# A graph convolution and attention kernel: attention moved from behind the second pass into it

## The chip, the cores and the metric

The kernel runs on one core of one Trainium2 chip. The metric is device time in microseconds (us). TensorE (PE) multiplies matrices, with its weight loads (PEld) shown apart; VectorE (DVE) and ScalarE (ACT) work on elements; GpSimd (POOL) issues the indirect transfers, that is gathers and scatters by a list of row numbers; SyncE (SP) and the queue of ACT issue the other transfers. Each engine works through its own list of instructions in order, and semaphores tie the lists together.

## The reference

N = 12500 nodes with D = 256 features, E = 200000 edges sorted by their destination. H = 4 heads of C = 64. Cut to what matters:

```
h = relu(layernorm(x))
h = h @ W_pre + b_pre                    # with a self loop added for each node:
h = relu(gcn(h, W1, b1)); h = relu(gcn(h, W2, b2))
x = x + h @ W_post + b_post
#   gcn(h): out[dst] += (h @ W)[src] * dinv[src] * dinv[dst];  + b
h = relu(layernorm(x)); xt = (h @ weight).reshape(N, 4, 64)
alpha_l = einsum('ehd,hd->eh', xt[src], attn_l)     # one score per edge and head
alpha_r = einsum('ehd,hd->eh', xt[dst], attn_r)
alpha = softmax(leaky_relu(alpha_l + alpha_r, 0.01), axis=1)      # over the 4 heads
tmp = einsum('nh,nhd->nd', alpha[:N], xt[dst[:N]])  # only the first N edges count
out = x + broadcast(tmp over the 4 heads)
```

So the attention needs, for each of the first 12500 edges, a score of its source, which can be any node, and the row of its destination. As the edges are sorted, the destinations of these edges are among the first nodes only (XW node tiles), while the sources spread over all 98.

## The kernel before

Edges are taken in tiles of 128 and chunks of J = 14 tiles: 112 chunks, 1563 tiles. Nodes are in NT = 98 tiles of 128.

A prologue normalises x, counts degrees, and writes the scaled rows to a table in DRAM. It also computes statistics of the rows of chunk 0 that were gathered raw from x (`raw_stats`, a bn_stats and a bn_aggr for each of 14 tiles).

Then `convolve` runs twice, once per graph convolution. For each edge tile POOL gathers the 128 source rows into a row buffer (L1397); for each chunk DVE makes a matrix of ones and zeros that marks the destinations (`fhot`, L1243); PE multiplies the two into the chunk's sum (`facc`, L1407). At the end of a chunk, `close` turns that sum and adds it to a moving buffer of node sums (L1288, L1208, L1305). A node tile whose sum is complete goes through `finish1` or `finish2`, whose steps are put off by a fixed number of edge tiles (the list at the end of `finish2`) and are carried out by `run(t)` after each tile. The order of every engine's list is thus written out by the loop over the tiles: what is emitted at tile t stands behind all that was emitted before.

In pass 1, chunks 0 to 3 were gathered raw in the prologue (RAW = 4; their statistics are taken one chunk ahead, at j = 9 of the chunk before), and chunks 4 to 27 are gathered as float32 rows of ftable. Meanwhile `split_rows` reads each node tile of that table back, splits it into three bf16 parts whose sum is the float32 value, and stores them (parts1). From chunk SINCE = 28 on, gathers take the parts and three bf16 matmuls do the work of a float32 one. Pass 2 takes parts for all chunks, from parts2, which `finish1` wrote. The row buffers of pass 2 are 4 of 9 tiles; those of the float32 part hold 14 tiles each. A gather into a row buffer waits until PE has multiplied what the buffer held before.

`finish2` ends with x after the two convolutions (fx, stored to kept_x by SP, L1563 and L1565), its normalised row, and the product with wg, which holds the attention weights (q, L1597): for node tiles under XW the whole row and its right score (table_r), for all the left scores, which ACT stores to table_l and table_e (r, L1605). table_e is table_l without the last three node tiles, so that the first chunk's gathers need not wait for them. During pass 2 `set_up` loads the sources and destinations that the attention starts with, and the rows of the first 14 tiles of the attention are multiplied out (`ends`, L1623).

The attention stands behind pass 2. It works on the 98 tiles of the first 12500 edges, in groups of G = 7. `ends_of` gets the destinations' rows by a product of a one-hot (`hot_t`, L1642) with rows that POOL gathered (`own_rows`, L1647): fends, L1741. `mix` has POOL gather the left scores of each tile's sources (fal, L1751), adds the scores that the three last node tiles lack in table_e (`missing`, L1722), takes the softmax (L1757 to L1767), weighs and sums the four heads on DVE (L1774 to L1781), adds the result to the kept x (fres, L1783) and stores it. The core of it:

```
for g in range(len(groups) + 2):
    if g < len(groups):
        keep(g)
        ends_of(g)
    if g >= 2:
        mix(g - 2)
```

Of the kernel before, what the change touches and what calls it, by code (L numbers as in the profile page):

```python
# [17 lines left out]
P = 128  # L18
# [395 lines left out]
def fast_path(  # L414
# [64 lines left out]
    assert AC * J == NT and AC * CE <= E and XW < NT  # L479
    table_r = dram.tile([XW * P, DR], F32, name="table_r")  # L480
    table_l = dram.tile([NT * P, H], F32, name="table_l")

    LW = 3
    table_e = dram.tile([NT * P, H], F32, name="table_e")
# [18 lines left out]
    base_b = const.tile([P, NCH], F32, name="base_b")  # L503
    row_i = const.tile([P, AC], I32, name="row_i")
# [88 lines left out]
    with tc.tile_pool(name="fprep", bufs=1) as prep:  # L593
# [233 lines left out]
        with tc.tile_pool(name="fpsum", bufs=2, space=PSUM) as psum, \  # L827
# [208 lines left out]
            raw_stats(0)  # L1036
            due.append((len(blocks), late))
            while n_stats < NG or due:
                if to_scale and to_scale[0] + 1 < n_stats:
                    scale(False)  # L1040
                one_more()
                fetch(2)
                if due:
                    norms(due.pop(0)[1])
# [10 lines left out]
            wide = prep.tile([NCH, P], F32, name="wide")  # L1055
            nc.vector.tensor_copy(wide, base.to_broadcast([NCH, P]))
# [7 lines left out]
            nc.tensor.matmul(fk[:, 2, :NCH], wide, ident[:NCH, :NCH], start=True, stop=True)  # L1064
# [7 lines left out]
            for f in after:  # L1072
                f()
            after = [raw_block(ends, m, psum.tile([P, 4 * P], F32, name="ft"), j0)
                     for j0 in (8, 12)]
            nc.vector.tensor_copy(base_b, fk[:, 2, :NCH])
            nc.vector.tensor_scalar(row_i, base_b[:, :AC], lane, float(XW * P - 1), op0=ALU.add,
                                    op1=ALU.min)
# [16 lines left out]
    def check_chunks(work, psum):  # L1095
# [20 lines left out]
        kept = work.tile([1, 1], F32, name="n_kept", bufs=1)  # L1116
        nc.vector.tensor_reduce(kept, pt[:1, 2, :NCH], AX.X, ALU.add)
        nc.vector.tensor_add(kept, kept, counted)
        nc.vector.tensor_scalar(bad_row, kept, -1.0, float(NCH + 1), op0=ALU.mult, op1=ALU.add)
# [12 lines left out]
    def load_late(pool):  # L1132

        nc.scalar.dma_start(roots, root_t)
        for t, w in ((wb, w2), (wo, w_post), (wg[:, :, :D], w_gat)):
            nc.scalar.dma_start(t, w.rearrange("(k p) n -> p k n", p=P))
        nc.scalar.dma_start(b2c, b2.rearrange("(k p) -> p k", p=P))
# [8 lines left out]
    def late_weights(pool, attn):  # L1146

        for i, ar in enumerate(attn):
            for k in range(KC):
                prod = pool.tile([P, H, C], F32, name="fprod", bufs=1)  # L1150
                nc.vector.tensor_mul(prod.rearrange("p h c -> p (h c)"), wg[:, k, :D], ar)
                nc.vector.tensor_reduce(wg[:, k, D + i * H:D + (i + 1) * H], prod, AX.X,
                                        ALU.add)

    def convolve(ep, table, stride, width, ahead, with_sum, psum, prepare, finish, parts, since,
                 lacking=False, raw=(), rows_p=None, behind=None):
# [35 lines left out]

        def new_buf():
# [24 lines left out]
        for n0 in range(0, BW, P):  # L1218
            v, n = {}, min(P, BW - n0)
            new_turned(v)  # L1220
            turn_sums(load_rows(n0, n), 0, v)
            nc.vector.tensor_copy(state["buf"][0][:, :, n0:n0 + n], v["pt"][:, :KC, :n])
            if with_sum:
                nc.vector.tensor_copy(state["buf"][1][:, n0:n0 + n], v["ps"][:, 0, :n])
# [6 lines left out]
        ready(0)  # L1231


        const_p = psum.tile([P, P if with_sum else P + D], F32, name="iota_p", bufs=1)
        iota_p = const_p[:, :P]
        nc.vector.tensor_copy(iota_p, iota_w)
        if not with_sum:
            state["bias"] = const_p[:, P:]
            nc.vector.tensor_copy(state["bias"], bob)

# [21 lines left out]
        def new_rows_of():  # L1262
            if with_sum:
                return new_got()
            return rows_p.tile([P, ONE, 3 * stride], BF16, name="fgot", bufs=ahead)

        def late_sums():
# [3 lines left out]
            froms = new_rows_of().rearrange("p j d -> p (j d)")[:, :J * D]  # L1271
            froms = froms.rearrange("p (j d) -> p j d", d=D)
            assert stride == TW * P and D == TW * P
            for i in range(TW):
                one_hots(froms[:, :, i * P:(i + 1) * P], from_0[:, i, :])
            px = psum.tile([P, KC, P], F32, name="fpt", bufs=1)
# [86 lines left out]
        def raw_ahead(c, j):  # L1363
# [4 lines left out]
            elif j in (3, 5, 7, 9):  # L1368
                raw_block(raw_lohi[c], raw_m[c], fpt(), 2 * (j - 3))()
                if j == 9:  # L1370
                    raw_stats(c)
# [5 lines left out]
        for t, (c, j) in enumerate(tiles):  # L1377
# [4 lines left out]
            if many == 1:  # L1382
                if j == 0:
                    gots = (raw + [spare])[c] if raw and c <= len(raw) else new_rows_of()
                got = gots[:, j, :]
            else:
                i = (t - since * J) % ONE
                if i == 0:
                    gots = new_rows_of()
                    if since:  # L1390
                        gots = gots.rearrange("p j d -> p (j d)").bitcast(BF16)
                        gots = gots[:, :ONE * 3 * stride].rearrange("p (j d) -> p j d", j=ONE)
                got = gots[:, i, :]
# [16 lines left out]
            if some and j == nj[c] - 1:  # L1410
                for i in range(TW):
                    nc.tensor.matmul(acc, late[0][:, i, :], late[1][i], start=False,
                                     stop=(i == TW - 1))
            if j == nj[c] - 1:
# [3 lines left out]
            if behind:  # L1418
                behind(t)
            run(t)  # L1420
        run()
# [51 lines left out]
    def split_rows(pool, psum):  # L1473
        rows = {}

        def load(w):
            rows[w] = pool.tile([P, D1], F32, name="frow", bufs=4)
            nc.sync.dma_start(rows[w], table1[w * P:(w + 1) * P, :])

        def step(t):  # L1480
# [3 lines left out]
            if k < NT:  # L1484
                load(k)
            if k >= 2:
                p = psum.tile([P, 4, P], F32, name="fpt", bufs=1)
# [354 lines left out]
```

## Time and profile before

| | us |
|---|---|
| three runs | 4912.08, 4915.13, 4934.78 (median 4915.13) |
| the profiled execution | 4877.83 |
| its span | 4875.9 |
| PE, PEld busy | 2648.6, 1780.7 |
| DVE, ACT busy | 1387.0, 614.7 |
| POOL busy | 3109.7 |
| granted TensorE clock, mean | 0.682 |

The span can be read in stages by the gather line. The first gather of pass 1 starts at 135.3 us, the first with parts at 674.9, the first of pass 2 at 2378.6, the last one at 4625.6. The attention's own gathers start at 4670.1. In the table of busy time by stretch each row gives a stretch, its length, and for every engine its busy time and number of instructions. In a row of the gather line stand the number of instructions, the least, median and largest duration in ns, and the first and last start in us. "issue" as a releaser is time in which the engine waited for nothing that the profile shows; "remote" is a releaser that it can't name. Below 0.5% of the time, two measurements can't be told apart.

### The profile page before, as it was taken

The numbers are of one execution on the slowest core, as the hardware profiler recorded it, in microseconds if no ns is written. First come the engines' busy times: TensorE is split into PE (matmuls) and PEld (weight loads), VectorE is DVE, ScalarE is ACT, GpSimd is POOL, SyncE is SP. The second block draws the span as 40 slices with busy tenths as digits, with TensorE's granted clock in tenths as the row PEclk, the third lists the DMA queues.
The fourth block names the chain that finished last, engine by engine and source line by source line (L and its number), as shares of the span: only waits on it lengthen the run. The fifth ranks groups of instructions, "written<-read, shape, count | busy, mean of one in ns | idle before, by whom it ended". The sixth has DMA issues, their size and how long they took to land. (4 is left out here: it accounts for less than half of the span.)

```text
span 4875.9 us, 38956 instructions
## 1 busy us (share of the span) xinstructions
PE 2648.6 (54%) x13306; PEld 1780.7 (37%) x13306; DVE 1387.0 (28%) x3009; ACT 614.7 (13%) x1625; POOL 3109.7 (64%) x3299
## 2 busy tenths in 40 slices
PE   5756555555555555555545555545455555545553
PEld 4534433233233333333333334333333343434341
DVE  7445532112122222222222222222222222212236
ACT  5212210000000000000001100010111101101011
POOL 7566646666666666666566666666666666666643
PEclk7766666666666666666666667666676766767766
DMA  8566655555555555555556666565566666656635
GB/s 269 147 178 184 191 157 154 159 158 161 163 156 161 158 162 157 160 157 163 147 157 177 162 159 155 158 161 151 154 159 160 157 156 156 163 153 158 159 110 155
DMA packets 413533, 787.28 MB, mean 161 GB/s; under 512 B 101005, under 2 KB 267172, under 8 KB 413324
## 3 DMA queue, kind: packets, MB, share of 16 engines
q0 software_dynamic: 197264, 594.53, 46.8%
q1 hardware_dynamic: 170214, 173.89, 11.4%
q10 hardware_dynamic: 45846, 16.27, 1.3%
q8 instruction: 107, 1.75, 0.2%
q14 instruction: 102, 0.84, 0.1%
HBM read 692.31 MB, written 92.05 MB: 161 GB/s over the span
## 5 line engine op out<-in xcount | busy, mean ns | idle before, releaser
L1397 POOL DMA_INDIRECT fgot<-parts,fsrc_t x2720 | 2580.2, 949 | 1372.9 <-issue 783.2
L1407 PE MATMUL facc<-fgot,fhot 128*128 128x256 bf16 (+2 forms) x8986 | 1743.4, 335 | 1152.0 <-issue 1105.8
L1407 PEld LDWEIGHTS <-fhot 128*128 128x128 bf16 x8202 | 902.3, 113 | 1593.5 <-issue 1399.0
L1243 DVE TENSOR_TENSOR fhot<-iota_p,to_t 128x1792 bf16<-128x1792 f32 (+1 forms) x224 | 449.2, 2005 | 8.0 <-remote 8.0
L1397 POOL DMA_INDIRECT fgot<-ftable,fsrc_t x336 | 318.8, 949 | 184.0 <-issue 104.2
L1468 DVE TENSOR_TENSOR fpo<-fpo,fparts 128x256 f32<-128x256 f32 x97 | 41.8, 431 | 922.8 <-ACT fo L1454 704.4
L1549 DVE SCALAR_TENSOR_TENSOR fy<-rb,fb2c,fpz 128x128 f32<-128x128 f32 x194 | 58.7, 344 | 850.4 <-remote 677.6
L1305 DVE TENSOR_TENSOR buf<-buf,fturn 128x256 f32 x224 | 94.4, 421 | 699.1 <-remote 510.0
L1558 PE MATMUL fpo<-fwo,fz 128*128 128x256 f32 x388 | 149.2, 523 | 200.1 <-ACT fz L1552 126.8
L1288 ACT ACTIVATE fsums<-facc 128x257 f32<-128x257 f32 (+1 forms) x224 | 85.2, 380 | 1326.9 <-remote 1122.2
L1563 DVE SCALAR_TENSOR_TENSOR fx<-fpo,fdinv,fxb 128x256 f32<-128x256 f32 x97 | 46.9, 483 | 643.4 <-remote 366.9
L1407 PEld LDWEIGHTS facc<-fgot,fhot 128*128 128x128 f32 x784 | 179.4, 237 | 131.2 <-issue 98.1
L1445 PE MATMUL fpo<-wf,buf 128*128 128x256 f32 x388 | 149.2, 496 | 125.5 <-issue 82.3
L1542 PE MATMUL fpz<-buf,fwb 128*128 128x128 f32 x776 | 137.4, 327 | 117.6 <-issue 99.5
L1558 PEld LDWEIGHTS fpo<-fwo,fz 128*128 128x128 f32 x388 | 91.3, 261 | 233.1 <-ACT fz L1552 142.6
L1208 PE MATMUL fturn<-fident,fsums 128*128 128x128 f32 x448 | 118.4, 348 | 100.2 <-issue 52.4
L1542 PEld LDWEIGHTS fpz<-buf,fwb 128*128 128x128 f32 x776 | 121.7, 236 | 127.4 <-issue 104.4
L1208 PE MATMUL fturn<-fident,self 128*128 128x128 f32 x396 | 106.6, 352 | 82.5 <-issue 46.7
L1445 PEld LDWEIGHTS fpo<-wf,buf 128*128 128x128 f32 x388 | 87.9, 248 | 161.5 <-issue 99.1
L1597 PE MATMUL fpx<-fwg,ht 128*128 128x4 f32 (+1 forms) x388 | 69.2, 286 | 129.9 <-ACT ht L1588 99.0
L1751 POOL DMA_INDIRECT fal<-table_l,fsrc_t x84 | 80.5, 958 | 69.3 <-DVE fs L1758 44.6
L1208 PEld LDWEIGHTS fturn<-fident,fsums 128*128 128x128 f32 x448 | 70.7, 177 | 144.8 <-issue 75.4
(284 smaller groups left out, 2272.8 us busy)
## 6 DMA issues: line engine op xcount, KB each, us to landing
fgot<-parts,fsrc_t POOLq DMA_INDIRECT x2720
parts<-frow_p SPq DMA_DIRECT2D x98, 195.0 KB
parts<-fparts SPq DMA_DIRECT2D x98, 192.0 KB
frow<-ftable SPq DMA_DIRECT2D x98, 130.0 KB
self<-ftable SPq DMA_DIRECT2D x99, 128.0 KB
self<-ftable SPq DMA_DIRECT2D x97, 130.0 KB
ftable<-fo ACTq DMA_DIRECT2D x98, 128.0 KB
kept_x<-fx SPq DMA_DIRECT2D x98, 128.0 KB
```

Of the source, the lines that this page charges most:

```text
L1208: nc.tensor.transpose(v["pt"][:, i * KC + k, :], rows[:, k * P:(k + 1) * P], ident)
L1243: nc.vector.tensor_tensor(h, iota_p[:, None, :].to_broadcast([P, n, P]), to[:, :, None].to_broadcast([P, n, P]), ALU.is_equal)
L1288: nc.scalar.activation(sb, acc, AF.Copy)
L1305: nc.vector.tensor_add(b, b, v["pt"][:, :KC, :])
L1397: nc.gpsimd.indirect_dma_start(out=got, out_offset=None, in_=rows_of[:(NT - TW) * P, :] if some else rows_of[:], in_offset=bass.IndirectOf ...
L1407: nc.tensor.matmul(acc, hots[c][:, j, :], got[:, i * stride:i * stride + width], start=(j == 0 and i == 0), stop=(j == nj[c] - 1 and i == ...
L1445: nc.tensor.matmul(po, buf[:, k, :P], wf[:, k, :], start=(k == 0), stop=False)
L1542: nc.tensor.matmul(pz[:, m, :], wb[:, k, m * P:(m + 1) * P], buf[:, k, :P], start=(k == 0), stop=(k == KC - 1))
L1549: nc.vector.scalar_tensor_tensor(y[:, m, :], v["root"], b2c[:, m:m + 1], v["pz"][:, m, :], op0=ALU.mult, op1=ALU.add)
L1558: nc.tensor.matmul(po, v["z"][:, m, :], wo[:, m, :], start=(m == 0), stop=(m == KC - 1))
L1597: nc.tensor.matmul(px, v["ht"][:, k, :], wg[:, k, d0:], start=(k == 0), stop=(k == KC - 1))
L1751: nc.gpsimd.indirect_dma_start(out=al[:, i, :], out_offset=None, in_=(table_l if c else table_e)[:], in_offset=bass.IndirectOffsetOnAxis(a ...
```

## The change

1. Prologue. The statistics of raw chunk 1 are taken in the prologue's last loop instead of in chunk 0 of pass 1. Two small results that only the old attention used (base_b, row_i) go. In pass 1 the first rows are loaded before chunk 0 as before, but turned and added (`begin_sums`, `ready(0)`) after its 14th tile.
2. Pass 1. `split_rows` has two row buffers instead of four and issues a tile's load after the store of the tile two before. When the split is done, `list_late` makes, out of the first N edges, a packed list of the late ones: those whose source is in node tile 84 or later (LATE), in up to 16 lists of 128. It writes to DRAM the sources modulo 128 (lo_rows), the destinations less each tile's first (rel_rows), the lists and the start rows. Its 62 parts stand two tiles apart.
3. Pass 2. The row buffers are 3 of 14 tiles. The tables table_l and table_e and their stores go: the left scores stay in SBUF (l_all). `attend` gives a list of items; `feed(t)` starts an item when the node tiles that it needs are finished and the item before has had its space of edge tiles, and puts its parts at tiles t, t + 1 and so on. The items: a load of the destination rows of each of the 98 tiles (`ends_of_tile`, a register read on SP and a transfer of 128 x 260 B); alpha_r by a one-hot of the destinations (14 items); one-hots and destination rows of the late lists, written to DRAM (4 and 16 items); alpha_l in five stages over the source tiles 0 to 18, 18 to 36, 36 to 54, 54 to 72 and 72 to 84, each of 14 items (a broadcast load of 229 KB, a one-hot of 128 x 896 on DVE, 21 bf16 matmuls with the scores as three parts, a mask, a product and a reduction on DVE). The first four stages' items stand four tiles apart. The items of the last stage go on to the end (`group`, ten tiles apart): softmax, shares as three bf16 parts, spread by matmuls with `pick`, weighed one-hots, 7 float32 matmuls that mix, the sum with kept x, and the store.
4. Behind pass 2 only the late edges remain. Their one-hots (1 MB) and rows (2 MB) are loaded into freed row buffers, POOL gathers their 16 x 128 rows of kept x, 16 matmuls give the left scores of the last 14 node tiles, then mask, softmax and mix, and POOL scatters the 16 lists of finished rows over those in the output.

The diff, cut to its core:

```diff
-                    raw_stats(c)                      # pass 1, j == 9
+                    if c > 1:
+                        raw_stats(c)
+                if known < 2:                         # prologue's last loop
+                    raw_stats(known)
+                    known += 1
...
+            if with_sum and t == J - 1:
+                begin_sums()
+                ready(0)
...
+        def feed(t):
+            if behind and t >= free_at[0] and behind[0][0]():
+                _, space, parts = behind.pop(0)
+                for i, part in enumerate(parts):
+                    if part:
+                        at(t + i, lambda _, part=part: part())
+                free_at[0] = t + space
...
-            return rows_p.tile([P, ONE, 3 * stride], BF16, name="fgot", bufs=ahead)   # ahead 4
+            return rows_p.tile([P, J, 3 * stride], BF16, name="fgot", bufs=ahead)     # ahead 3
...
-            rows[w] = pool.tile([P, D1], F32, name="frow", bufs=4)
+            t = pool.tile([P, G * P], BF16, name="list_h", bufs=2)
+            rows[w] = t.bitcast(F32)[:, :D1]
...
-            nc.scalar.dma_start(table_l[w * P:(w + 1) * P, :], xa[:, DR:])
-            if w < NT - LW:
-                nc.scalar.dma_start(table_e[w * P:(w + 1) * P, :], xa[:, DR:])
+            nc.scalar.activation(l_all[:, w, :], v["px"][:, DR - d0:], AF.Copy)
+            mark("w", w)
...
+        def ends_of_tile(t):
+            at = start_of(t, (XW * P - NB) * H)
+            nc.sync.dma_start(ends[:, t, :], by_head[bass.ds(at, P), :])
...
+            def product():                             # alpha_r
+                for j in range(G):
+                    nc.tensor.matmul(v["p"][:, j, :], v["h"][:, j * P:(j + 1) * P],
+                                     v["r"][:, j, :], start=True, stop=True)
...
+            def load():                                # alpha_l
+                v["row"] = row_of(lo_rows, b, "lo_all", 1)
+            def equal():
+                v["h"] = new_hot().bitcast(BF16)[:, :HE]
+                nc.vector.scalar_tensor_tensor(v["h"], v["row"], 0.0,
+                                               banks["lane"].to_broadcast([P, HE]),
+                                               op0=ALU.subtract, op1=ALU.is_equal)
+            def product():
+                p = bank()[:, :G * nw * H]
+                for j in range(G):
+                    for i in range(3):
+                        nc.tensor.matmul(p[:, j * nw * H:(j + 1) * nw * H],
+                                         v["h"][:, j * P:(j + 1) * P], l_parts[s][:, i, :],
+                                         start=(i == 0), stop=(i == 2))
+            def taken():
+                nc.vector.tensor_tensor(mask, ..., ALU.is_equal)
+                nc.vector.tensor_tensor(v["p"], v["p"], mask..., ALU.mult)
+                nc.vector.tensor_reduce(some, v["p"].rearrange("p t w h -> p t h w"), AX.X, ALU.add)
+                nc.vector.tensor_add(al[:, t, :], al[:, t, :], some)
+            return [load, None, equal, product, taken]
...
+            return [load, None, equal, product, taken, lambda: v["soft"][0](),      # group
+                    lambda: v["soft"][1](), split, turn, turned, over(0, 4), weigh(0, 4), over(4, G),
+                    weigh(4, G), mix, end]
...
+        for b in range(NG):
+            items.append((when("w", XW), 4, alpha_r(b)))
+        for b in range(KL // 4):
+            items.append((when("w", XW), 6, late_hots(b)))
+        for k in range(KL):
+            items.append((when("w", XW), 4, late_ends(k)))
+        for s in range(len(STAGES) - 1):
+            items.append((when("w", STAGES[s][1]), 2, l_of_stage(s)))
+            for b in range(NG):
+                items.append((when("w", STAGES[s][1]), 4, alpha_l(s, b)))
+        items.append((when("w", LATE), 2, l_of_stage(len(STAGES) - 1)))
+        for b in range(NG):
+            items.append((when("w", LATE), 17 if b + 1 == NG else 10, group(b)))
...
-        for g in range(len(groups) + 2):               # behind pass 2: keep, ends_of, mix
...
+        for k in range(KL):                            # behind pass 2: late edges only
+            nc.tensor.matmul(z[k // 8][:, k % 8, :, :], sets["hot"][:, k * P:(k + 1) * P],
+                             l_all[:, LATE:, :], start=True, stop=True)
...
+            for i in range(k0, k0 + n):
+                nc.gpsimd.indirect_dma_start(
+                    out=out[:], out_offset=bass.IndirectOffsetOnAxis(ap=late_i[:, 0, i:i + 1],
+                                                                     axis=0),
+                    in_=sets["x"][:, i, :], in_offset=None)
```

## The prediction

> **What bounds the kernel now.** I read the page first (busy shares, the chain, the groups), then the gather line by pass, then busy time by stretch, then the chain and the groups of the last 208 us.
>
> The page of the profile: engines, and the group that fills most of the span.
>
> ```profile
> span 4875.9 us, 38956 instructions
> PE 2648.6 (54%) x13306; PEld 1780.7 (37%) x13306; DVE 1387.0 (28%) x3009; ACT 614.7 (13%) x1625; POOL 3109.7 (64%) x3299
> ...
> L1397 POOL DMA_INDIRECT fgot<-parts,fsrc_t x2720 | 2580.2, 949 | 1372.9 <-issue 783.2
> ```
>
> No engine is full, yet one row covers most of the time: 2720 gathers, 949 ns each. The gather line alone, in pass 1's float32 part and in pass 2 (duration ns min/median/max, first and last start; then idle us, times):
>
> ```profile
> L1397 POOL DMA_INDIRECT fgot<-ftable,fsrc_t x336: 941/949/1191, 135.3 to 629.3; - x168
> ```
>
> ```profile
> L1397 POOL DMA_INDIRECT fgot<-parts,fsrc_t x1549: 941/949/1641, 2396.1 to 4625.6; - x194
> ...
>   issue: 445.1, 1460
>   remote: 245.2, 73
> ```
>
> Pace: (629.3 - 135.3) / 335 = 1.475 us per gather in the float32 part, (4625.6 - 2396.1) / 1548 = 1.440 in pass 2. Between neighbours POOL idles 445.1 / 1460 = 0.305, so an unhindered gather is 0.949 + 0.305 = 1.254 us. The rest, 0.186 x 1549 = 288 us, is the 73 waits of 3.4 us and their like, where POOL wants a row buffer that PE has not freed. Pass 2 is therefore POOL's line with PE close behind it. Busy time by stretch (PE, PEld, DVE, ACT, POOL; then clock, DMA share, GB/s):
>
> ```profile
> 400.00:675.00 275.00, 166.36 (x542) 119.38 (x543) 151.97 (x344) 66.35 (x186) 152.95 (x163) 0.70 0.64 179
> 1200.00:1700.00 500.00, 267.38 (x1320) 159.70 (x1321) 109.54 (x206) 39.37 (x100) 328.99 (x348) 0.65 0.58 159
> 3000.00:3500.00 500.00, 261.67 (x1510) 189.63 (x1510) 111.68 (x240) 50.33 (x139) 328.21 (x347) 0.70 0.60 156
> 4650.00:4876.00 226.00, 96.59 (x335) 61.80 (x335) 117.11 (x232) 41.17 (x117) 94.18 (x98) 0.64 0.45 138
> ```
>
> To be seen: 347 and 348 gathers per 500 us in both passes, though pass 2 issues 14% more matmuls (1510 against 1320). In pass 2 PE is busy 52%, DVE 22%, ACT 10%. The last row is the attention behind the passes, where nothing overlaps a gather. Its chain (start us, us) and its groups:
>
> ```profile
> 4668.73 1.37 DMA table_l<-fxl
> 4677.59 5.94 DMA fal<-table_e,fsrc_t
> ...
> 4725.94 8.77 PE lacks L1722 x42
> ...
> 4836.61 4.82 DMA fal<-table_l,fsrc_t
> ```
>
> ```profile
> L1751 POOL DMA_INDIRECT fal<-table_l,fsrc_t x84 | 80.5, 958 | 69.3 <-DVE fs L1758 44.6 <-issue 24.7
> L1741 PE MATMUL fends<-rows,hot_t 128*128 128x260 f32 x168 | 68.8, 552 | 92.9 <-issue 58.3 <-ACT fxg L1743 34.0 <-ACT fxl L1605 0.3
> ...
> L1774 DVE TENSOR_TENSOR near<-fxg,share 128x896 f32<-128x896 f32 (+2 forms) x13 | 13.2, 1015 | 0.4
> ...
> L1777 DVE TENSOR_TENSOR some<-near,far 128x448 f32<-128x448 f32 (+2 forms) x15 | 8.8, 590 | 0.5
> ```
>
> From 4668.7, when the last tile's scores are stored, to 4875.9: 207 us. The sum below is made against the profiled execution (4877.8 us, 1.9 outside the span). It lies 37.3 us (0.8%) under the median of the runs, 4915.1; I add the change to the median.
>
> **The tail, 207 us removed.** 98 gathers of fal (98 x 1.25 = 123 us of POOL), 84 fends, the lacks and 15 mixes go from behind the passes. What stands there afterwards, in series behind the same last scores:
> - z: 16 float32 products 128x56. The lacks chain gives 8.77 us for 42 records, at four records (weights and matmul, two each) 0.84 us a product of 4 columns; fends 0.55 x 2 = 1.1 at 260. Sixteen at 0.84 are 13; records missing from that chain could halve it. I take 10.
> - Two mask products (448 elements, 0.59 as in some) and two reductions at the same: 2.4.
> - Softmax: seven small DVE steps of 0.2, the exponential 0.2, some 0.4 of handing over, perhaps a table load: 3.5.
> - First pair of lists: three DVE steps of 512 elements, 0.6 each: 1.8. The other 14 lists (about 12 us of DVE) run beside the scatters.
> - 16 scatters of 128 rows to the output. In POOL's order each waits for the landing of the one before, as all write the same tensor. No scatter is in this trace. Bounds: 1.25 each if the wait were free (20 us); the slowest gather to landing, 5.94 each (95). I take the last gather of the tail, alone on its queue, 4.82 from start to landing: 77. It is the nearest row, a small indirect transfer with nothing behind it.
> Sum 95 instead of 207: **-112**; bounds -170 and -92. The 16 row gathers and the 3 MB of loads start when the ring drains, beside the last tile's 40 us chain (4626.5 to 4668.7), so they cost nothing; if that cover failed, 3 MB at 156 GB/s are 20 us.
> The Trainium skill, "DMA: Bandwidth & Descriptors", section on the anatomy of one DMA, puts about 2.0 us of fixed cost on a DMA from POOL, most of it the receipt of the write. By that estimate a scatter takes 0.95 + 2.0 + 0.3, 16 take 52, and the tail gains 137 instead of 112; the sum above keeps 77.
>
> **Pass 2, what is added under the gathers.** 98 small loads with an SP register each, 14 alpha_r, 4 late_hots, 16 late_ends, 56 alpha_l four gathers apart, 14 groups ten apart.
> - DVE, per alpha_l: the one-hot of 896 (1.0, as near), mask 0.2, product and reduction of 504 (0.6 each), sum 0.1: 2.5. Four gathers last 5.76 us and hold 4 x 111.68/347 = 1.3 of DVE already; 3.8 fits. Over the pass: 70 x 2.5 + 14 x 1.4 + 14 x 5 = 265 us, 12 points of load. Cost 0; the cover is DVE's idle 34% there. alpha_l has one buffer for its broadcast row (229 KB), refilled once the last one-hot has read it, some four gathers ahead; a load that is 2 us later than that leaves DVE waiting, the chunk's hot matrix (needed some 12 gathers on) behind it, and then PE.
> - PE, per alpha_l: 21 bf16 products of 72 columns. A weight load is 113 ns in the page's mean for this form, a matmul of PE's mix 261.67/1510 = 173: between 2.4 and 3.6 us. PE idles 4 x (1.440 - 261.67/347) = 2.7 us in four gathers. So between nothing and 0.9 us over; I take 0.25, nearer the weight load since 72 columns are few, x 70 = 18. alpha_r: 7 float32 pairs of about 0.5 are 3.5 against 2.7, 0.8 x 14 = 11. Groups: 28 x 0.13 + 7 x 0.5 = 7.1 against 6.9 in ten gathers: 3. Behind each item's products stand the next tile's facc products, and behind those POOL's buffer. With 8 for the late items, **+40**. Bounds: 0, as the 14% more matmuls of pass 2 cost no pace; in series, 70 x 3.6 + 14 x 3.5 + 14 x 7 = 400.
> - ACT: exponentials among square roots, 28 table loads at 1.28 (the tail's one) are 36 us in an engine that is 10% busy. 0.
> - Ring of 3 x 14 rows instead of 4 x 9: the nearest row with 14-row buffers is the float32 part, 0.035 slower, x 1562 = +54 at most; below, the 288 us of waits. I take 0, since the deeper float32 ring stood no better. The 190 small stores of scores that go were on ACT's queue, in nobody's way: 0.
> - The Trainium skill, "SBUF — State Buffer", section "Who interferes with whom", speaks against this move: a DVE operation with two SBUF inputs or in a two-port mode shuts out GpSimd (in the first case one that reads SBUF) for its whole length. The row says otherwise: the gather's median is 949 ns in the float32 part, with DVE busy 55%, and 949 in pass 2 at 22%. By the page, if all of the added DVE work locked POOL out, the sum would be up to 265 us worse.
>
> **Prologue and pass 1.** raw_stats(1), 14 x 0.40 and 14 x 0.14 = 7.5 us of DVE, moves ahead of pass 1; DVE is busy 101 of 136 us there: between -7.5 and +7.5, taken 0. The first sums move behind 14 tiles, with loads issued as before. The list of late edges: 14 x 2.1 + 12 = 41 us of DVE and 98 products over 124 gathers (180 us); DVE is 55% busy at most, bounds 0 and 41, taken +5. split_rows with two row buffers: loads go out after the stores on SP, six gathers (8.8 us) ahead of use: 0, at worst 10.
>
> Sum: -112 + 40 + 5 = **-67**; profiled 4811, median **4848**.
>
> **Rivals.**
> - A, the items are hidden altogether (for it: pace equal at 1320 and 1510 matmuls; against: 21 products in four gathers more than double PE's count there): -112 + 5 = 4808; with scatters that do not wait, 4750.
> - B, PE is the limit in the alpha windows (for it: POOL's 73 waits are for PE; against: 48% idle): 70 items cost 2.6 to 3.6 each, 182 to 252; 4915 - 107 + 182 to 252 = **4990 to 5060, slower**. It decides when pass 2 grows by more than 107 us, 1.5 us per item, a mean pace of 1.509.
> - C, the new ring ends half of POOL's waits: -144 more, about 4690.
> - D, growth and gain cancel: 4890 to 4940.
>
> **How the numbers follow.** A measurement here can tell about 0.5% (25 us) from nothing. Forecast (growth 15 to 85): 0.42, its own range 4815 to 4890. A 0.23, C 0.04, D 0.09, B 0.22. Faster 0.69, same 0.09, slower 0.22. The range runs from 4720 (leaves out C and little of A) to 5010 (leaves the upper half of B).
>
> **What would show it.** Last gather to end: 250 before, about 138 after; scatter starts 4.8 apart (1.25: A's end). Gather pace of pass 2 between 1.45 and 1.50 over the alpha windows and 1.44 before them; near 2.1 there would be B. POOL's waits still on PE; DVE near 35% in pass 2. Wrong if DVE waits for the broadcast rows, if late pieces of attention stand behind the last gather, or if the first 700 us move by more than 20.

## The result, and the profile after

The changed kernel takes 5127.12 us (median of 4 runs, 5125.84 to 5130.85) against 4913.6 for the kernel before (4910.49 to 4934.78): a ratio of 1.0418, 95% interval 1.0397 to 1.044. It is 213 us slower; 4848 had been forecast. The profiled execution took 5126.9 us, 249 more than that of before.

In later sets of runs the kernel before takes either 4153 to 4159 us or 4878 to 4884 us, one and the same chip gave 4153.7 in one set and 4877.9 in another, and the first measurement is of the second kind. I call the two conditions quick and slow by the rate at which PE starts its instructions, which is where they differ; the time of the kernel before in each set says which it was.

The gather line of the changed kernel in pass 2, to be held against the one of before:

```profile
L1424 POOL DMA_INDIRECT fgot<-parts,fsrc_t x1549: 940/946/962, 2417.6 to 4986.4; - x194
...
  issue: 449.3, 1459
  PE facc L1434: 447.2, 42
  remote: 138.6, 43
```

A gather takes what it took (946 ns), but the gathers' waits now make 628 us of pass 2 (2586.3 less 1562 x 1.254) instead of 288, and most of those with a name are for PE. The first gather of pass 2 starts at 2400.1 (2378.6 before), the last at 4986.4 (4625.6), and the span ends at 5125.1 (4875.9). So the 249 us are +21.5 up to pass 2, +339.4 in pass 2 (2586.3 against 2246.9), and 138.7 instead of 250.4 behind the last gather, -111.7.

Busy time by stretch of the changed kernel (columns as in the rows of before):

```profile
2420.00:3000.00 580.00, 286.56 (x1593) 210.92 (x1594) 120.69 (x246) 51.45 (x156) 342.22 (x362) 0.67 0.54 149
3500.00:4000.00 500.00, 260.14 (x1783) 201.05 (x1783) 157.50 (x324) 46.37 (x130) 293.95 (x312) 0.69 0.52 150
4500.00:5000.00 500.00, 277.61 (x1830) 217.36 (x1831) 195.36 (x458) 64.54 (x149) 248.17 (x263) 0.67 0.59 178
```

In 500 us there are 312 and then 263 gathers instead of 347, while PE is busy for hardly more of the time than before (49 to 56%, 52% before) at the same granted clock. DVE, at 21 to 39%, is not the bound either. PE is neither full nor done early. Over pass 2 as a whole (kernel before, changed kernel):

```profile
2378.60:4625.60 2247.00, 1196.66 (x6778) 852.11 (x6778) 518.32 (x1081) 225.08 (x615) 1483.70 (x1564) 0.70 0.61 159
2400.10:4986.40 2586.30, 1362.69 (x8659) 1034.79 (x8658) 782.87 (x1665) 261.06 (x718) 1476.37 (x1563) 0.68 0.55 157
```

PE's busy time grew by 166 us and pass 2 by 339, so half of the growth is time in which PE stands still. What it waits for shows in the list of PE's waits in pass 2 (us in total, times, longest); first the kernel before, then the changed one:

```profile
PE facc L1407 <- issue: 457.8, 511, 3.1
PE fpo L1558 <- ACT fz L1552: 126.3, 26, 15.5
PE fpz L1542 <- issue: 99.5, 42, 10.1
```

```profile
PE facc L1434 <- issue: 306.0, 284, 3.3
PE behind L2071 <- issue: 162.0, 79, 10.3
PE fX L1830 <- issue: 138.7, 90, 4.6
PE behind L2071 <- DVE hot_s L2063: 85.9, 30, 9.2
```

"issue": PE stands still and nothing that the profile knows of holds it. The trace of before shows how, in the order of time (the rows of PE and of its weight loads):

```profile
3144.41 0.37 PE L1407 MATMUL facc<-fgot,fhot 128*128 128x256 bf16 x1 [1.73 <-issue]
3144.41 0.18 PEld L1584 LDWEIGHTS fpt<-fident,h 128*128 128x128 f32 x1 [1.30 <-issue]
3145.10 0.37 PE L1584 MATMUL fpt<-fident,h 128*128 128x128 f32 x1 [0.32 <-issue]
3145.12 0.18 PEld L1584 LDWEIGHTS fpt<-fident,h 128*128 128x128 f32 x1 [0.52 <-issue]
3146.50 0.37 PE L1584 MATMUL fpt<-fident,h 128*128 128x128 f32 x1 [1.03 <-issue]
3147.22 0.10 PEld L1407 LDWEIGHTS <-fhot 128*128 128x128 bf16 x1 [1.92 <-issue]
3147.22 0.39 PE L1407 MATMUL facc<-fgot,fhot 128*128 128x256 bf16 x1 [0.35 <-issue]
```

Starts are 0.70 us or a multiple of it apart (3144.41, 3145.10, 3146.50, 3147.22), whatever the instruction is, where a gather's matmuls are mostly 0.11 or 0.21 us apart otherwise. Counted over pass 2, such stretches last some 10 us. Most begin 10 to 15 us after POOL has resumed its gathers and end some 4 us after the last gather before POOL's next stop for a row buffer. So behind most stops of POOL, PE gets through some 110 to 150 recorded instructions, and then 0.70 us or more pass for each further one.

### The profile page after: what moved, and what is told of

It is laid out like the page before. It is cut to its first block, busy times and chain, and to the rows that moved or that the text cites. A ratio compares the mean times of both kernels' runs of the same rounds, so it can differ in the third digit from the quotient of the medians.

```text
span 5125.1 us, 43794 instructions
## 1 busy us (share of the span) xinstructions
PE 2742.8 (54%) x15210; PEld 1947.4 (38%) x15210; DVE 1625.3 (32%) x3575; ACT 623.5 (12%) x1643; POOL 3029.2 (59%) x3226
## 5 line engine op out<-in xcount | busy, mean ns | idle before, releaser
L1434 PEld LDWEIGHTS <-fhot 128*128 128x128 bf16 x8202 | 920.0, 116 | 1362.2 <-issue 1150.5
L1830 PE MATMUL fX<-buf,fwb 128*128 128x128 f32 x776 | 168.8, 363 | 177.6 <-issue 138.7
L1851 DVE SCALAR_TENSOR_TENSOR fx<-fX,fdinv,fxb 128x256 f32<-128x256 f32 x97 | 46.8, 483 | 621.9 <-remote 270.9
L2071 PE MATMUL behind<-l_parts,hot_s 128*128 128x72 bf16 (+1 forms) x1470 | 88.1, 223 | 248.8 <-issue 162.6
L1837 DVE SCALAR_TENSOR_TENSOR fy<-rb,fb2c,fX 128x128 f32<-128x128 f32 x194 | 58.5, 343 | 511.3 <-remote 447.1
L1830 PEld LDWEIGHTS fX<-buf,fwb 128*128 128x128 f32 x776 | 144.7, 268 | 188.4 <-issue 141.9
L1233 PE MATMUL fturn<-fident,fsums 128*128 128x128 f32 x448 | 122.0, 362 | 128.5 <-ACT fsums L1319 70.3
L2071 PEld LDWEIGHTS <-hot_s 128*128 128x128 bf16 x1470 | 72.7, 116 | 271.9 <-issue 174.4
L1846 PE MATMUL fX<-fwo,fz 128*128 128x256 f32 x388 | 126.1, 457 | 66.6 <-ACT fz L1840 64.7
L1885 PE MATMUL fY<-fwg,ht 128*128 128x4 f32 (+1 forms) x388 | 75.2, 303 | 144.6 <-issue 74.4
```

Source lines behind the costliest of these rows:

```text
L1233: nc.tensor.transpose(v["pt"][:, i * KC + k, :], rows[:, k * P:(k + 1) * P], ident)
L1434: nc.tensor.matmul(acc, hots[c][:, j, :], got[:, i * stride:i * stride + width], start=(j == 0 and i == 0), stop=(j == nj[c] - 1 and i == ...
L1830: nc.tensor.matmul(pz[:, m, :], wb[:, k, m * P:(m + 1) * P], buf[:, k, :P], start=(k == 0), stop=(k == KC - 1))
L1837: nc.vector.scalar_tensor_tensor(y[:, m, :], v["root"], b2c[:, m:m + 1], v["pz"][:, m, :], op0=ALU.mult, op1=ALU.add)
L1846: nc.tensor.matmul(po, v["z"][:, m, :], wo[:, m, :], start=(m == 0), stop=(m == KC - 1))
L1885: nc.tensor.matmul(px, v["ht"][:, k, :], wg[:, k, d0:], start=(k == 0), stop=(k == KC - 1))
```

## The experiments

In the tables, "pass 2" is from the first to the last start of its gathers, and "end" from there to the end of the span, all from the profiled executions.

**One part alone, and the whole without attention.** The ring of the changed kernel put into the kernel before:

```diff
-            return rows_p.tile([P, ONE, 3 * stride], BF16, name="fgot", bufs=ahead)   # 4 x 9
+            return rows_p.tile([P, J, 3 * stride], BF16, name="fgot", bufs=ahead)     # 3 x 14
```

> The kernel before with one part of the change alone: the row buffers of pass 2 are 3 of 14 tiles instead of 4 of 9. Pass 2 of before lasts 2247 us from its first to its last gather (1.440 us per gather), that of the changed kernel 2586. If the ring costs what it costs the float32 part (1.475 per gather, one wait of about 3 us per 14 gathers), pass 2 becomes 2300, +54. If the ring is what makes the changed kernel's gathers 100 to 300 of pass 2 slow (1.56, before any attention item but the first), pass 2 becomes about 2430, +185. If only the items are to blame, it stays at 2247.

The changed kernel without its attention:

```diff
-        items.append(...)              # all of them
-                 behind=attend(psum), at_end=tail_begins, consts=give2,
+                 behind=attend(psum), consts=give2,
-    (the late edges behind pass 2)
+        nc.sync.dma_start(out[:, :], kept_x[:N, :])
```

> The changed kernel without any attention: no items in pass 2, nothing behind it but a copy of kept x to the output, so the attention's part of the result is left out. Ring of 3 x 14, shared PSUM banks fX and fY, list of late edges stay. If the items cost all of the 339 us that pass 2 grew by, pass 2 lasts 2250 to 2300. If the ring and the shared banks cost 0.12 us per gather, 2430. The first gather of pass 2 stays at 2400 (2379 before) either way, since the prologue and pass 1 are the changed kernel's.

One of three parts in the alpha_l products:

```diff
-                    for i in range(3):
-                        nc.tensor.matmul(..., l_parts[s][:, i, :], start=(i == 0), stop=(i == 2))
+                    nc.tensor.matmul(..., l_parts[s][:, 0, :], start=True, stop=True)
```

> The changed kernel with one of the three bf16 parts in the alpha_l products: 7 matmuls per item instead of 21, so the left scores lose two of their parts. If PE's matmul count in these items is the cost, 70 x 14 matmuls of 0.12 to 0.17 us less are 118 to 167 us less in pass 2. If the cost is per item (PE waiting for the one-hot, the one-hot for the row), pass 2 falls by less than 50 us.

All three fell where the kernel before takes 4153.7: 4168.4, 4041.4 and 4126.5 us. Pass 2 lasted 1956.7, 1953.0 and 1960.5, that is 1.25 us per gather, the pace that the prediction had called unhindered. None of the expectations for the slow condition was tested, as POOL hardly waited for PE in any. But 4126.5 against 4153.7 for a kernel that holds nearly all of the change turned the question round: is the change slower at all where PE does not crawl?

**The change itself, and its items spread.**

> The changed kernel itself, unchanged. In the first set of runs the kernel before took 4153.74 us on its chip, not 4913, and its relatives had a gather pace of 1.250 us in both passes with hardly a wait of POOL for PE. If the change's loss of 213 us hangs on PE's slow stretches, then on such a chip it is faster than before, by about the tail's 112 us less the 77 of late work that shows, some 4125 against 4154; on a chip where before takes 4910, it takes 5125 again. If the loss is in the kernel's own order, it is slower by 150 or more on either.

Measured 4125.73 us (4123.01 to 4130.29) against 4153.66 of before: ratio 0.993, interval 0.9913 to 0.9946. **The same kernel is 0.7% faster in the quick condition and 4.2% slower in the slow one.** Its pass 2 is 1966.6 us with all items in it, and behind the last gather it takes 130.0, where the run with the old attention (ring alone) took 163.8. Its PE waits in pass 2:

```profile
PE facc L1434 <- DMA fgot<-parts,fsrc_t: 467.8, 515, 4.0
PE behind L2071 <- DVE hot_s L2063: 125.9, 54, 6.4
```

No "issue" any more: PE waits for the gathered rows, 515 times, that is for POOL, and has time to stand in the items for DVE. The second line matters: in the quick condition PE waits even longer for the one-hots (125.9 us against 85.9) and it costs nothing.

```diff
-                items.append((when("w", STAGES[s][1]), 4, alpha_l(s, b)))
+                items.append((when("w", STAGES[s][1]), 10, alpha_l(s, b)))
```

> The changed kernel with the items of the first four alpha_l stages 10 gathers apart instead of 4. Where PE has slow stretches (pace of before 1.44): if PE is saturated inside the dense windows, pass 2 falls by 60 to 120 us from 2586; if every item costs a hand-over whatever its distance, it stays within 30 us. Where the pace is 1.250 throughout, no difference over 10 us.

4124.87 us, as the changed kernel: nothing to be had where all is hidden. (Fourteen gathers apart, planned before this, gave no result.)

**Is it PE's time as such?** To make PE the bound in the quick condition, zero matmuls were added per edge tile of pass 2:

```diff
+            if not with_sum and j:
+                for i in range(6):                     # later 12
+                    nc.tensor.matmul(acc, nothing, got[:, :width], start=False, stop=False)
```

> The kernel before with six matmuls against a zero weight matrix added per edge tile in pass 2 (all but the first tile of a chunk), which add nothing to the sum and only load PE, so that PE and not POOL sets the pace of pass 2, as it seems to do where the kernel takes 4910. On a chip where the pace is 1.250: PE's 0.80 us per gather plus 6 x 0.14 to 0.17 gives 1.6 to 1.8 us per gather, pass 2 of 2500 to 2800 us.

> The changed kernel with the same six matmuls per edge tile. If the loss comes from PE work added to a pass in which PE sets the pace, the changed kernel's pass 2 is now longer than that of the kernel before with the same load by about the work that it adds: 1470 products at 0.12 to 0.16, 98 and 98 float32 ones at 0.5, the late ones: 280 to 350 us, near the 339 of the first measurement; slower in all by 150 to 230. If the loss has another cause (the ring, waits for loads), pass 2 grows by less than 100 here and the changed kernel stays the faster one.

> The changed kernel without attention (no items, nothing behind pass 2 but a copy of kept x to the output) with the same six matmuls per edge tile: it has the ring of 3 x 14 and the shared PSUM banks only. If these cost anything where PE sets the pace, pass 2 is longer than that of the kernel before with six by up to 100 to 200 us; if the items alone cost, the two agree within 30 us.

Six were too few, against the expectation: PE was then 92% busy at a clock of 1.00 and still kept up. 4161.2, 4150.2 and 4051.4 us, pass 2 of 1957, 1987 and 1956. So in the quick condition PE can carry 8700 more matmuls (6 x 1451 tiles), several times the items' number, in the time of the gathers. Twelve were enough:

> The kernel before with twelve zero matmuls per edge tile in pass 2. With six, PE was 92% busy at a clock of 1.00 and still hidden behind the gathers (1.250 us each, 0.107 to 0.125 us per matmul). Twelve are 0.65 us more per gather: PE sets the pace, 0.92 x 1.25 + 6 x 0.107 = 1.8 us per gather, pass 2 of about 2800 us.

> The changed kernel with the same twelve. If the first measurement's loss is the PE time of the items in a pass whose pace PE sets, pass 2 is longer than with the kernel before by the items' own PE time at a warm clock: 1470 products at 0.107 are 157, the 210 float32 and 114 other products another 100 to 150: 250 to 310 us, against 339 there, and the whole is slower by 120 to 240. If items cost because PE waits in them for DVE or a load, it is longer by clearly more than 339; if PE has nothing to do with it, by less than 100.

> The same with one of the three bf16 parts in the alpha_l products (two parts of the left scores left out): 980 matmuls fewer, at 0.107 these are 105 us less in pass 2 than with three parts, if matmuls are what the items cost; under 30 us less if it is the hand-overs.

| twelve zero matmuls | whole | pass 2 | end |
|---|---|---|---|
| kernel before | 4918.8 | 2656.1 | 215.1 |
| changed | 4952.4 | 2763.6 | 148.2 |
| changed, one part | 4919.6 | 2732.9 | 148.7 |

One stretch of the changed kernel with twelve:

```profile
2400.00:3000.00 600.00, 600.00 (x5604) 542.29 (x5603) 171.07 (x360) 62.86 (x182) 308.97 (x327) 1.00 0.54 148
```

PE is busy in 600.00 of 600 us. There the items, with the ring and the shared banks, cost 107.5 us, and the 980 matmuls of two parts 30.7 us, 0.031 us each. The trace says the same: the 21 products of an item start 0.031 us apart in the mean, whether the one-hot is the one of the product before or a new one. The expectation (250 to 310, and 105) was far too high; 107.5 is near the "less than 100" that it gave for causes other than PE's time. So with PE full, the change loses 0.7% (one run each). The 339 us by which pass 2 grew in the first measurement are not the time that PE computes: as shown above, its busy time there grew by 166.

**The slow condition again.** The kernel without attention was run once more, and the condition had come back:

> The changed kernel without attention once more (a copy of kept x stands for it), for a chip or an hour in which the kernel before takes 4910 and PE has slow stretches. There the first measurement has 1.56 us per gather in gathers 100 to 300 of pass 2, before any item of weight, against 1.44: if the ring and the shared banks cost this all along, pass 2 lasts about 2430 (of 2247 before, 2586 with the items); if those 200 gathers are no measure, 2250 to 2300. Where before takes 4153 again, pass 2 lasts 1953 as it did.

The kernel before took 4884.3, this one 4790.1, with a pass 2 of 2309.2. Over its pass 2:

```profile
2396.60:4705.80 2309.20, 1223.92 (x6740) 876.12 (x6739) 510.54 (x1068) 219.75 (x609) 1480.81 (x1563) 0.67 0.54 153
```

A second set in the slow condition, with the kernel before at 4877.9, holds three more kernels:

> The changed kernel with one of three parts in the alpha_l products, 980 matmuls and 980 weight loads fewer (two parts of the left scores left out). Where before takes about 4900: in the first measurement these products held PE's line for 339 us of pass 2 (from each instruction's start to the next one's). If the matmul count is the cost, two thirds of 339, some 150 to 220 us, go from pass 2 of 2586; if the waits at the item's start are the cost (200 us of the 339 stood before an item's first product), it falls by under 80. Where before takes 4153, no change against 4126.

> The changed kernel with the items of the first four alpha_l stages 10 gathers apart instead of 4. Where before takes about 4900: if the items only hurt where they stand too dense for PE, pass 2 falls by 60 to 150 us; if each item costs its time at any distance, it stays within 30 us. Where before takes 4153, no change against 4125.

The third of them has one part and four buffers of 11 tiles:

```diff
-            return rows_p.tile([P, J, 3 * stride], BF16, name="fgot", bufs=ahead)      # 3 x 14
+            return rows_p.tile([P, 11, 3 * stride], BF16, name="fgot", bufs=ahead)     # 4 x 11
```

> The changed kernel with one part in the alpha_l products and a ring of 4 buffers of 11 tiles instead of 3 of 14. Where before takes about 4900: one wait of about 3 us per 14 gathers becomes one per 11 or, as with the buffers of 9, one per two buffers; if the ring's grain made the 62 us that pass 2 lasts longer without attention, these go, and with the part's gain the whole is at or below the kernel before (4880 to 4915). If not, it stands with the run that has one part alone, within 20 us. Where before takes 4153, no change against 4126.

| slow condition | whole | pass 2 | end | gathers 300-462 | 462-1415 | 1415-1562 |
|---|---|---|---|---|---|---|
| kernel before | 4877.8 | 2246.9 | 250.4 | 234 | 1374 | 212 |
| changed | 5126.9 | 2586.3 | 138.7 | 297 | 1538 | 298 |
| without attention | 4790.1 | 2309.2 | 82.6 | 242 | 1416 | 213 |
| one part | 5037.2 | 2516.5 | 135.4 | 294 | 1490 | 288 |
| ten apart | 5067.2 | 2540.1 | 141.6 | 291 | 1519 | 290 |
| one part, 4 x 11 | 4942.4 | 2416.7 | 138.1 | 267 | 1446 | 271 |

The last three columns are lengths in us of stretches of pass 2, by the number of the gather: loads, alpha_r and late edges; the four spread alpha_l stages; the groups. Each row is one execution, and the rows come from three sets, in which the kernel before took 4910 to 4935 (changed), 4884.3 (without attention) and 4877.9 us (the last three); its row is the profiled execution of 4877.8. How far rows differ by themselves can be seen where they are the same kernel: the first 300 gathers of pass 2 take 454 us in the changed kernel and 440 with the items ten apart, which differ only later. So differences of some 30 us between rows of different sets say nothing, and the kernel before itself differs by more than the 0.5% that was taken for the limit. What follows:
- Ring and shared banks cost 62 us without any item, against the 54 of the upper bound; which of the two was not parted. A wait of 3.7 us in the mean, mostly per 14 gathers, takes the place of one of 3.1 us per 18.
- The items cost the other 277: 55 in the first stretch, 122 over the 56 alpha_l items (2.2 us each), 85 over the 14 groups (6.1 us each), 15 elsewhere. PE's busy time rises by 139 of the 277 (1362.69 less 1223.92); in the other 138 PE stands still.
- Leaving out 980 matmuls with their weight loads takes 70 us off pass 2, 0.07 us each against 0.031 in a full PE. In the changed kernel an item's products start 0.089 us apart in the mean (0.040 in the quick condition, 0.031 in a full PE), so an instruction costs PE's line more here than its time. Yet 70 lies on the side that the expectation gave to the waits at an item's start (under 80), and the trace agrees: the time within the items' products falls from 124 to 21 us, the time before their first ones rises from 217 to 252.
- Spreading the items takes 46 us off pass 2, but 28 of them stand in stretches that the edit leaves as they are (454 to 440, 297 to 291, 298 to 290). That it saves anything is not shown.
- The finer ring, on top of one part, saves another 100 in the same set, more than the 62 that it was to win back; the whole still stays above the 4880 to 4915 that were expected then. It also works on the stretches in which one part changed little (294 to 267, 288 to 271).

Where PE's line of pass 2 goes can be added up from the trace, each PE instruction's share being the time from the start of the one before it, so that a wait counts for what ends it. In the changed kernel the items hold 593 us of it (alpha_l products 339, alpha_r 62, shares 62, late rows 60, mixes 41, the rest 29), in the same kernel in the quick condition 337. That these 339 equal the growth of pass 2 is chance. The 337 fit beside the gathers there, since PE waits for rows anyhow; in the slow condition POOL waits for PE already without them.

**Two more edits.** In the first, the products of an alpha_l item stand three gathers behind its one-hot instead of one:

```diff
-            return [load, None, equal, product, taken]
+            return [load, None, equal, None, None, product, taken]
```

> The changed kernel with the products of the alpha_l items of the first four stages three gathers behind their one-hots instead of one. Where before takes about 4880: if PE loses its time waiting for the one-hots (86 us of waits named so, 200 us before the items' first products), pass 2 falls from 2586 by 50 to 120 us; if those 200 us are only PE's slow stretches, which would stand before some other instruction otherwise, it stays within 30 us. Where before takes 4153, no change against 4125.

> One part in the products, 4 buffers of 11 tiles, the first four stages' items ten gathers apart, their products three gathers behind the one-hots. Where before takes about 4880: one part and the ring gave a pass 2 of 2417; if the other two add their 20 to 50 us each, 2320 to 2380, and with a tail of 138 instead of 250 the whole is 4845 to 4905, level with before; if they overlap, it stays at 2400 to 2420 and at about 4930, slower by 1%. Where before takes 4153, about 4120, 0.8% faster, as the changed kernel.

> The four edits together once more (one part in the products, 4 buffers of 11 tiles, items ten apart, products three gathers behind the one-hots). Where before takes about 4880: pass 2 of 2320 to 2380 and 4845 to 4905 in all if the last two edits add to the first two, 2400 to 2420 and about 4930 if they overlap. Where before takes 4153, about 4120 again.

All fell in the quick condition. 4122.6 us for the products alone; the four edits together 4119.81 (ratio 0.9924, interval 0.9908 to 0.9941) and 4123.55 (0.9929, 0.9912 to 0.9945). They beat the kernel before by 0.7% and are level with the changed kernel. What the hand-over to DVE costs in the slow condition, and whether the four edits together reach the kernel before there, is open: no run of them fell there. The best that was measured there, one part and 4 x 11, is 1.3% slower than before (4942.4 against 4877.9, one run each).

## Why the prediction was wrong

It named the loss (rival B: PE is the limit, slower, decided by pass 2 growing over 107 us; it grew by 339), gave it 0.22, and priced it at 4990 to 5060. The forecast, the range and the sign were wrong.

- **The pace and who waits for whom** were read rightly: POOL waits for PE, 288 us of it in pass 2. What was not asked is why PE, 52% busy, is late. The page of before has the answer in one row:

```profile
L1407 PE MATMUL facc<-fgot,fhot 128*128 128x256 bf16 (+2 forms) x8986 | 1743.4, 335 | 1152.0 <-issue 1105.8
```

 Of 1152 us idle before these matmuls, 1106 end with "issue" and hardly any with the landing of the rows. In the quick condition the same row reads

```profile
L1434 PE MATMUL facc<-fgot,fhot 128*128 128x256 bf16 (+2 forms) x8986 | 1866.7, 351 | 904.5 <-DMA fgot<-parts,fsrc_t 880.0
```

- **The step that failed is PE's room in pass 2.** It took the idle 2.7 us in four gathers as free for the items' products, and +40 in all. With attention alone added, the items cost 277 (pass 2 of 2309.2 without and 2586.3 with them, one execution each). Idle time that ends with "issue" was no room; work put into it lengthened the line, and by twice the 139 us of PE's busy time that it added. The row of the alpha_l products in the changed kernel has both, 88 us busy and 249 idle before them:

```profile
L2071 PE MATMUL behind<-l_parts,hot_s 128*128 128x72 bf16 (+1 forms) x1470 | 88.1, 223 | 248.8 <-issue 162.6
```

 The support for it, the same pace at 1320 and at 1510 matmuls, was a true reading that did not carry from 14% to twice the number.
- **The price of a product** was wrong the other way: 0.11 to 0.17 us from rows of other shapes, where the row above has 0.060 busy for each (88.1 us for 1470) and a full PE 0.031. Rival B's 182 to 252 us came from it. Its side was right and its mechanism half right: of the 277, 139 are PE's busy time, and in the rest PE stands still. That it came out on this side is in part the luck of the condition: in the quick one its 107 us are not nearly reached.
- **The ring** was taken at 0, with +54 as the bound: 62 measured, with the shared banks. Of the two rows at hand, the float32 part's pace was the right one.
- **The sign "wrong if DVE waits for the broadcast rows"** was seen, but it does not explain the loss: DVE waits for them 28.8 us in pass 2 (19 times), and in the quick condition 70.3 us (41 times), where it costs nothing.
- **The tail**, -112, came out at -111.7, but by luck, as a sum of errors that cancel. A scatter follows the one before by 2.9 us, not 4.82: the 16 take 46.7 us from the first one's start to the last one's landing (5068.2 to 5114.9), 30 less than the 77. The chain from the last gather to the last scores takes 67.6 us (4986.4 to 5054.0) instead of 42, with the last group and the last tiles standing together there, and 10.2 us pass between the last landing and the end of the span, for which the sum had no term. In the quick condition the part behind the last gather shrinks by 34 us only (163.8 to 130.0). That the scatters wait for one another was right:

```profile
L2303 POOL DMA_INDIRECT out_dram<-fgot,late_i x16 | 15.6, 972 | 34.0 <-DMA out_dram<-fgot,late_i 24.6 <-DVE fgot L2300 7.2 <-DVE tail_mix L2298 2.2
```

 The price of the Trainium skill, "DMA: Bandwidth & Descriptors", section on the anatomy of one DMA, was nearer: with its figure of about 2.0 us of fixed cost the estimate was 3.25 a scatter, against the 2.9 measured.
- **Prologue and pass 1** were taken at +5; the first gather of pass 2 is 21.5 later here, and 5 to 18 later in the four other runs of the slow condition; in the quick one it starts at 2027 to 2039 with the changed prologue and pass 1 and at 2038 to 2046 with those of before. The cause was not tested.
- **The lock of the shared port**, of which the Trainium skill speaks in "SBUF — State Buffer", section "Who interferes with whom", did not show: in a pass 2 with DVE up to 39% busy the gather's median is 946 ns and its longest 962, as the rows of before had said (median 949).
- **Rival A**, everything hidden, and what C guessed, an end of POOL's waits, are what pass 2 of the quick condition shows (1966.6 us with the items, 1956.7 with the ring alone in the kernel before), though not by the ring. C's own 4690 was added up wrongly: 4848 less 144 is 4704.

## What to carry to other kernels

Before counting an engine's idle time as room, look at what ends it. If it ends with data or with another engine, work can be put there; if it ends with "issue", as here, the engine itself may be the slow part, and what is added to it can lengthen the line by more than its own duration. A price for a small operation taken from rows of another shape can be several times off in either direction, so a change whose sign hangs on it deserves a run that loads the engine until it is full. And a kernel that is tuned to an engine's limit can change sides when the condition of the chip does: compare it in each, against the kernel before in the same set.

## What had not been expected of the hardware

- PE starts instructions 0.70 us or a multiple of it apart for some 10 us at a time while gathers flow, and this condition comes and goes between sets on one chip; the kernel before takes 18% longer in it (4878 to 4915 against 4153). DMA packets take the same time in both: the median of a gather's packets in pass 2 is 175 ns, and that of the 16 KB packets of the instruction queue whose number grows with PE's list (122 in the changed kernel, 258 with twelve zero matmuls) is 1.0 us, so a slower fetch of instructions does not show either. Why PE does so was not settled. Every time on record comes with the profiler's clock and span, so whether the recording of PE's many instructions has a part in it stays untested as well.
- In the quick condition the granted clock rises with the load: 0.73 over the span of the changed kernel, and 0.96 to 1.00 in the stretches of pass 2 with six and with twelve zero matmuls.
- A 72-column product costs 0.031 us in a full PE at a clock of 1.00, with a weight load recorded for each, and no more where the one-hot is a new one.
